# A fused attention and feed-forward kernel: the root's table loaded ahead of the keys' squares, prompt types moved behind a rotation, last products kept in PSUM

## The chip, the cores and the metric

One core of a Trainium2 chip. The metric is the device time of one execution in microseconds; several runs of the kernel are compared by their median. The engines are named TensorE (PE), VectorE (DVE), ScalarE (ACT), POOL (GpSimd) and SyncE (SP); each works through its own instructions in order, and they wait for each other by semaphores.

## The reference

`x` is 64 sequences of 64 tokens of 256 numbers. Cut to what matters:

```python
# block 1: rotate, linear attention with decay, residual
c, s = a * cos(ang), a * sin(ang)          # a = amplitudes ** delta, ang = frequencies * delta
out0, out1 = c * x0 - s * x1, s * x0 + c * x1     # pairs of token rows
q, k, v = split((out @ W_qkv.T).reshape(B, L, 3, 16, 16))   # 64 sequences, 64 tokens, 16 heads of 16
k = (k - mean(k)) * rsqrt(var(k) + 1e-5)   # over each head's 16 numbers
S = sigmoid(log_gamma) * S + v k^T;  y = S q   # scan over the tokens, per head
x = x + y @ W_o.T
# block 2: pooled by a softmax whose mask depends on the prompt type, then a quantized feed-forward
scores = tanh(x @ W1 + b1) @ v
mask = prefix if type == 0 else postfix if type == 1 else all but self
p = softmax(where(mask, scores, -1e30));  pooled = (p @ x) / count(mask)
xq = round(pooled / sx) * sx               # one scale for the whole tensor; weights: one per row
h = quantized(silu(xq @ Wg.T) * (xq @ Wu.T))
x = x + h @ Wd.T
```

## The kernel before

The 4096 tokens are 32 tiles of 128 tokens; four tiles make a group, and there are eight groups (`NG = 8`). All of `x` stays in SBUF. The order of the instructions on TensorE, ScalarE, VectorE and POOL is the order of the code (a schedule written out by hand); SyncE issues most DMAs.

**Preparation.** Constants are built, weights of the attention are turned by TensorE into `wqT`, `wkT`, `wvT`, `woT`, and group 0 is brought up to its scores. `scale_ys(g)` multiplies a group by the sine (POOL, except for group 0), `rotate(g)` adds the cosine part (VectorE, eight instructions, L182 and L185). `gneg`, `gexp`, `gln`, `lgam` make the logarithm of the decay from `log_gamma`; two VectorE products (L777) and an exponential (L788) make the table of decays `gam`. The prompt types of the sequences (`tib`, integers) become numbers `tf` (L756), three selectors `sel` (L761 to L764) and the counts `cnt` (L765, L767): nine VectorE instructions. Nothing of block 2 is needed before the loop.

**Loop over groups.** Pass `p` (1 to 7) projects group `p` and finishes the attention of group `a = p - 1`, while group `q = p - 2` has its pooling. `transposed` copies the transposed inputs from PSUM (ScalarE, L215). `keys(p)` makes the keys on TensorE (`pk`, L225), squares them on ScalarE (L241) and sums the squares per head on VectorE (L242, `ssq`). `weighted` and `diagonal` make `py` and `yT` of group `a` (L384, L400 on ScalarE, L401 on VectorE), `scores` and `decay` make `psc` (L342) and `at` (L367). `key_root(p)` takes the square root on ScalarE (L255), `hidden(q)` a tanh there (`th`, L465), `key_norm(p)` normalises the keys on VectorE (L261 to L273, `kn`), `queries(p)` makes `pq` on TensorE (L302) and `qbd` on ScalarE (L310), `token_scores(q)` makes `psr`, `output` makes `po` (L411), `residual` adds it (L422). Square root and tanh lie in different tables of ScalarE; a load is an instruction of its own, placed by the compiler ahead of the activation that needs another table, unless the code asks for it earlier. Most products live in four PSUM banks that are handed on as their readers finish: `pa` and the first half of `pq` take the banks that the two halves of `yT` are read from, the second half of `pq` takes the bank of `pa` once `th` has read it, `psr` that of the first `pq`, `po` that of the keys' first half once `kn` has read it. In pass 1, where there is no `pa`, the two halves of `pq` take the two banks of `yT`.

**Feed-forward.** After the loop the pooled values are quantized, gate and up products made in a fixed order of steps, then quantized again; `down(g)` multiplies by the down weights into `pdn` (L1229), VectorE applies the scale (L1238) into `res`, the group's result in SBUF. For groups 4 to 7 (`plain`) the residual is added on chip (L1247), by POOL for groups 4 to 6 and by VectorE for group 7, and written out by SyncE (L1248); groups 0 to 3 go out by an adding DMA of POOL's queue (L1251). Group 7 ends with one piece of two tiles and two of one.

Of the kernel before, what the change touches and what calls it, by code (L numbers as in the profile page):

```python
# [15 lines left out]
ALU = mybir.AluOpType  # L16
AX = mybir.AxisListType

P = 128
# [8 lines left out]
def adaln_attn_ffn(  # L28
# [20 lines left out]
    nc = tc.nc  # L49
    B, S, D = x.shape  # L50
# [6 lines left out]
    NN = NT // P  # L57
# [3 lines left out]
    NG = NN // GT  # L61
# [22 lines left out]
    cs, sel, cnt = c32("cs", 2, NN), c32("sel", 3, NN), c32("cnt", NN)  # L84
# [13 lines left out]
    dsc = const.tile([P, D], F32, name="dsc")  # L98
# [22 lines left out]
    with ExitStack() as actx:  # L121
# [37 lines left out]
        def scale_ys(g):  # L159
            if g == 0:  # L160

                ys = pool.tile([P, GT, D], F32, tag="ys", name="ys_0", bufs=1)
                for t in range(GT):
                    nc.scalar.activation(
                        ys[:, t], xg[0][:, t], AF.Copy, scale=cs[:, 1, t : t + 1]
                    )
                T["ys", g] = ys
                return
            tn = slice(g * GT, (g + 1) * GT)
            ys = pool.tile([P, GT, D], F32, tag="ys", name=f"ys_{g}", bufs=1)  # L170
            nc.gpsimd.tensor_tensor(  # L171
                ys, xg[g], cs[:, 1, tn].unsqueeze(2).to_broadcast([P, GT, D]), ALU.mult
            )
            T["ys", g] = ys

        def rotate(g):

            xs, ys = xg[g], T.pop(("ys", g))
            xr = pool.tile([P, GT, D], F32, tag="xr", name=f"xr_{g}", bufs=1)
            for t in range(GT):  # L180
                c = cs[:, 0, g * GT + t : g * GT + t + 1]
                nc.vector.scalar_tensor_tensor(  # L182
                    xr[:, t, 0:P], xs[:, t, 0:P], c, ys[:, t, P:D], ALU.mult, ALU.subtract
                )
                nc.vector.scalar_tensor_tensor(  # L185
                    xr[:, t, P:D], xs[:, t, P:D], c, ys[:, t, 0:P], ALU.mult, ALU.add
                )
            T["xr", g] = xr
# [45 lines left out]
        def keys(g):  # L234

            ssq = pool.tile([P, GT * NH], F32, tag="ssq", name=f"ssq_{g}")
            pks = []
            for r in range(2):
                pk = by_token(g, r, wkT, "pk")
                sq = pool.tile([P, 512], F32, tag="sq", name=f"sq_{g}_{r}")  # L240
                nc.scalar.activation(sq, pk, AF.Square)  # L241
                nc.vector.tensor_reduce(  # L242
                    ssq[:, r * 2 * NH : (r + 1) * 2 * NH],
                    sq.rearrange("p (h e) -> p h e", e=E),
                    AX.X,
                    ALU.add,
                )
                pks.append(pk)
            T["pk", g] = pks, ssq
# [331 lines left out]
        with tc.tile_pool(name="prep", bufs=1) as prep:  # L581
            V = nc.vector

            def p32(name, *free):
                return prep.tile([P, *free], F32, name=name)
# [5 lines left out]
            tib = prep.tile([P, B], I32, name="tib")  # L591
# [16 lines left out]
            for k in range(2):  # L608
                rows = slice(k * A, (k + 1) * A)
# [13 lines left out]
            for k in range(P // 32):  # L623
                rows = slice(32 * k, 32 * (k + 1))
                V.tensor_scalar_add(row[rows], sq32[rows, 0:1], 32.0 * k)
            V.tensor_scalar(ident, col, row, None, ALU.is_equal)
            for k in range(2):
                rows = slice(k * S, (k + 1) * S)
# [20 lines left out]
            lag, npre = p32("lag", S), p32("npre", 2)  # L649
# [14 lines left out]
            rows = bank("rows")  # L664
# [73 lines left out]
            w, pt = turned(wkT, wq_nat, center, 2)  # L738
# [4 lines left out]
            first_transposed(0)  # L743
            w, pt = turned(wqT, wq_nat, ident, 0)
            first_transposed(1)
            V.tensor_copy(w, pt)

            gneg, gexp, gln, lgam = (
                p32(n, NH) for n in ("gneg", "gexp", "gln", "lgam")
            )  # L750
            V.scalar_tensor_tensor(gneg, lgb, -1.0, lgb, ALU.mult, ALU.min)

            tf = p32("tf", NN)
            for k in range(2):
                rows = slice(k * S, (k + 1) * S)
                V.tensor_copy(  # L756
                    tf[rows].rearrange("p (u k) -> p u k", k=2),
                    tib[rows].rearrange("p (u c k) -> p u c k", c=2, k=2)[:, :, k, :],
                )

            V.tensor_single_scalar(sel[:, 0, :], tf, 0.0, ALU.is_equal)  # L761
            V.tensor_single_scalar(sel[:, 1, :], tf, 1.0, ALU.is_equal)
            V.tensor_add(sel[:, 2, :], sel[:, 0, :], sel[:, 1, :])
            V.tensor_scalar(sel[:, 2, :], sel[:, 2, :], -1.0, 1.0, ALU.mult, ALU.add)  # L764
            V.tensor_scalar_mul(cnt, sel[:, 2, :], float(S - 1))  # L765
            for k in range(2):
                V.scalar_tensor_tensor(  # L767
                    cnt, sel[:, k, :], npre[:, k : k + 1], cnt, ALU.mult, ALU.add
                )
            nc.scalar.preload_act_table_set("natural_log_exp_and_others")  # L770
            nc.scalar.activation(gexp, gneg, AF.Exp)
            nc.scalar.activation(gln, gexp, AF.Ln, bias=1.0)
# [22 lines left out]
            w, pt = turned(wvT, wq_nat, ident, 4)  # L795
# [8 lines left out]
                V.tensor_scalar_mul(vb[half, half], ones[half, half], v1s[half])  # L804
            V.tensor_copy(w, pt)
            rotate(1)
            scale_ys(2)
            values(0)
            keys_transposed(0)
# [72 lines left out]
        for step in range(1, NG):  # L882
            p, a, q = step, step - 1, step - 2
            scores(a, 0)
            decay(a, 0)
            if q > 0:
                pooling_out(q - 1)
            T["xT", p] = transposed(T.pop(("xr", p)), p, "xT")
            if q >= 0:
                T["x2T", q, both] = transposed(xg[q], q, "x2T")  # L890
            if p + 1 < NG:
                rotate(p + 1)
                if p + 2 < NG:
                    scale_ys(p + 2)
            keys(p)
            weighted(a, 0)
            diagonal(a, 0)
            scores(a, 1)
            decay(a, 1)
            key_root(p)  # L900
            if q >= 0:
                hidden(q)
            key_norm(p)
            queries(p)
            if q >= 0:
                token_scores(q)
                softmax_exp(q)
            output(a, 0)
            residual(a, 0)
            weighted(a, 1)  # L910
            diagonal(a, 1)
            if q >= 0:
                softmax_div(q)
            mask_bias(a)
            if step == 1:

                nc.scalar.activation(csig, clips, AF.Sigmoid)
            if step < 4:
                weight_scale(step - 1)
            values(p)  # L920
            keys_transposed(p)
            if step < 4:
                weight_round(step - 1)
            if q >= 0:
                weights_transposed(q)
            if 2 <= step < 5:
                weight_widen(step - 2)
            output(a, 1)
            residual(a, 1)
            if q >= 0:  # L930
                pooling(q)
            if 2 <= step < 4:
                weight_transpose(step - 2)
# [76 lines left out]
    with ExitStack() as fctx:  # L1010
# [203 lines left out]
        def down(g):  # L1214
            j, k = divmod(g, 2)

            plain = g >= NG // 2
            res = xg[g - NG // 2 if plain else g]
            at = 0
            for r in range(2):  # L1220
                tiles = slice(2 * r, 2 * r + 2)

                for n in (1, 1) if g == NG - 1 and r else (2,):
                    pdn = ps_d.tile([P, n, D], F32, tag="pdn", name=f"pdn_{g}_{at}")
                    for i in range(n):
                        tok = slice((at + i) * P, (at + i + 1) * P)
                        for c in range(NC):
                            last = c == NC - 1
                            nc.tensor.matmul(  # L1229
                                pdn[:, i, :],  # L1230
                                hq[j][:, NF if last else 2 * c + k, tok],
                                wdT[:, c + k if last else c, :],
                                start=(c == 0),
                                stop=(c == NC - 1),
                            )
                    some = slice(at, at + n)
                    at += n
                    nc.vector.tensor_tensor(  # L1238
                        res[:, some],
                        pdn,  # L1240
                        dsc.unsqueeze(1).to_broadcast([P, n, D]),
                        ALU.mult,
                    )
                    if plain:
                        xr = xg[g][:, some, :]
                        by = nc.gpsimd if g < NG - 1 else nc.vector
                        by.tensor_tensor(xr, xr, res[:, some], ALU.add)  # L1247
                        nc.sync.dma_start(out=ot[g][:, some, :], in_=xr)  # L1248
            if not plain:

                nc.gpsimd.dma_start(out=ot[g], in_=res, accum_op=ALU.add)  # L1251
# [53 lines left out]
```

## Time and profile before

| | |
|---|---|
| runs | 301.86, 301.82, 301.11 us, median 301.82 |
| profiled execution | 301.5 us, span 299.5 us, granted clock 0.998 |
| busy share of the span | TensorE 94%, VectorE 77%, ScalarE 67%, POOL 30% |
| attention loop, passes 1 to 7 | about 28 to 199 us of the span, 24.7 to 25.9 us a pass from pass 2 on |
| down products | about 275.5 to 294.3 us |

The span runs from the first to the last instruction of the profiled execution; 2.0 us lie around it. A line of a timeline gives the start, the time taken, the engine, the line of the code, the operation, output and inputs, and in square brackets how long the engine stood idle before it and who ended that. Where several instructions are merged, `x2` and the like tell how many.

### The profile page before, as it was taken

The page shows a single profiled execution, that of the slowest core. Times are in us where ns is not written, and L with a number is a line of the kernel's source. Part 1 is how long each engine was busy: PE and PEld are TensorE (multiplying, and loading weights), DVE is VectorE, ACT ScalarE, POOL GpSimd, SP SyncE. Part 2 cuts the span into 40 slices and gives each one's busy share as a digit, 9 for nine tenths or more (in the row PEclk, how much of TensorE's full clock was granted, in tenths as well). Part 3 has the DMA queues.
Part 4 walks back from the last instruction along what each step waited for, and adds up shares of the span by engine and source line. Part 5 has one row for each costly group of instructions (what it writes and reads, how often), then busy time and mean ns, then how long its engine had stood idle before and what let it go on. Part 6 is the DMA issues. An engine that isn't in the chain of part 4 may idle for free.

```text
span 299.5 us, 8823 instructions
## 1 busy us (share of the span) xinstructions
PE 280.3 (94%) x3818; PEld 201.7 (67%) x3824; DVE 230.3 (77%) x496; ACT 200.2 (67%) x303; POOL 90.0 (30%) x83
## 2 busy tenths in 40 slices
PE   6999999999999999999999999999879999967993
PEld 5967778668858857875885885777534444434882
DVE  6788885876997697498489557746678999995875
ACT  2785368657684875466358447453489999959990
POOL 0232510600150060045100400016104758850693
PEclk9999999999999999999999999999999999999999
DMA  6596402001000200200000000000000000000796
GB/s 202 158 326 198 143 2 73 2 2 51 25 2 0 74 2 2 71 5 3 0 2 2 2 4 2 0 5 2 2 3 0 0 3 0 0 0 2 109 216 237
DMA packets 14860, 14.50 MB, mean 48 GB/s; under 512 B 1766, under 2 KB 14566, under 8 KB 14822
## 3 DMA queue, kind: packets, MB, share of 16 engines
q1 hardware_dynamic: 12706, 11.84, 12.1%
q0 software_dynamic: 2112, 2.10, 4.7%
q8 instruction: 30, 0.49, 0.7%
q14 instruction: 8, 0.07, 0.1%
q10 hardware_dynamic: 4, 0.00, 0.0%
HBM read 7.65 MB, written 6.29 MB: 47 GB/s over the span
## 4 chain that ended last, share of the span: by engine, by line
PE 74%; ACT 14%; DVE 9%; issue 2%; POOL 0%; POOLq 0%; ACTq 0%; DVEq 0%
PE pv L225 10%; PE po L411 9%; PE pk L225 8%; PE py L384 6%; PE pdn L1229 6%; PE pg L1116 5%; PE pq L302 5%; PE pu L1116 5%; PE psc L342 4%; ACT L255 3%; PE pl L547 3%; ACT L465 3%; PE pxT L212 2%; PE pkT L289 2%; PE idle L659 2%
## 5 line engine op out<-in xcount | busy, mean ns | idle before, releaser
L367 DVE TENSOR_TENSOR at<-psc,gam 128x512 f32<-128x512 f32 x62 | 38.5, 683 | 12.2 <-PE psc L342 12.2
L171 POOL TENSOR_TENSOR ys<-x,cs 128x1024 f32<-128x1024 f32 x7 | 13.3, 1893 | 99.3 <-DVE xr L185 83.5
L302 PE MATMUL pq<-xT,wqT 128*128 128x512 f32 x64 | 31.1, 613 | 1.8 <-ACT th L465 1.8
L411 PE MATMUL po<-woT,yT 128*128 128x256 f32 x128 | 30.2, 380 | 0.0
L225 PE MATMUL pv<-wvT,xT 128*128 128x256 f32 x128 | 29.8, 386 | 0.2 <-ACT qbd L310 0.2
L225 PE MATMUL pk<-wkT,xT 128*128 128x256 f32 x128 | 29.2, 381 | 0.2 <-ACT xT L215 0.2
L225 PEld LDWEIGHTS pv<-wvT,xT 128*128 128x128 f32 x128 | 23.7, 190 | 4.7 <-issue 1.2
L411 PEld LDWEIGHTS po<-woT,yT 128*128 128x128 f32 x128 | 23.7, 190 | 3.5 <-ACT qbd L310 0.5
L225 PEld LDWEIGHTS pk<-wkT,xT 128*128 128x128 f32 x128 | 23.5, 190 | 3.7 <-ACT xT L215 0.9
L1145 DVE TENSOR_REDUCE ham<-hT 128x1 f32<-128x1024 f32 (+1 forms) x25 | 25.9, 1085 | 0.1
L1127 ACT ACTIVATE gate<-pg,wsx 128x1024 f32<-128x1024 f32 (+1 forms) x25 | 25.0, 1013 | 1.3 <-PE pg L1116 1.0
L310 ACT ACTIVATE qbd<-pq,hm 128x512 f32<-128x512 f32 x32 | 20.1, 683 | 8.0 <-PE pq L302 8.0
L1138 POOL TENSOR_TENSOR hT<-gate,up 128x1024 f32<-128x1024 f32 x10 | 23.5, 2362 | 5.5 <-ACT up L1132 5.5
L1116 PE MATMUL pu<-xq,wuT 128*128 128x512 bf16 (+1 forms) x94 | 22.9, 379 | 1.2 <-DVE hT L1140 1.1
L1116 PE MATMUL pg<-xq,wgT 128*128 128x512 bf16 (+1 forms) x94 | 23.0, 381 | 1.0 <-DVE xq L1052 0.9
L1229 PE MATMUL pdn<-wdT,hq 128*128 128x256 bf16 x192 | 22.0, 273 | 2.0 <-DVE hq L1052 1.9
L302 PEld LDWEIGHTS pq<-xT,wqT 128*128 128x128 f32 x64 | 11.0, 189 | 17.8 <-issue 8.6
L1229 PEld LDWEIGHTS <-hq 128*128 128x128 bf16 x192 | 18.3, 98 | 5.9 <-DVE hq L1052 3.8
L400 ACT ACTIVATE yT<-py,hm 128x256 f32<-128x256 f32 x32 | 13.4, 470 | 11.3 <-PE py L384 11.3
L401 DVE SCALAR_TENSOR_TENSOR yT<-py,hm,yT 128x256 f32<-128x256 f32 x32 | 14.0, 480 | 8.7 <-ACT yT L400 8.4
L342 PE MATMUL psc<-qbd,kT 32*64 32x128 f32 x1024 | 20.2, 279 | 0.5 <-ACT kT L292 0.3
L241 ACT ACTIVATE sq<-pk 128x512 f32<-128x512 f32 x16 | 9.5, 596 | 16.0 <-PE pk L225 16.0
(203 smaller groups left out, 556.1 us busy)
## 6 DMA issues: line engine op xcount, KB each, us to landing
x<-in_x_dram SPq DMA_DIRECT2D x7, 512.0 KB, 7.3
out_dram<-x SPq DMA_DIRECT2D x4, 512.0 KB, 4.7
out_dram<-x POOLq DMA_DIRECT2D x4, 512.0 KB, 6.9
out_dram<-x SPq DMA_DIRECT2D x7, 256.0 KB, 4.1
wq_nat<-in_L_attn_W_qkv_dram SPq DMA_DIRECT2D x3, 256.0 KB, 4.0
wnat_d<-in_L_ffn_w_down_dram SPq DMA_DIRECT2D x1, 704.0 KB, 6.3
wnat<-in_L_ffn_w_gate_dram SPq DMA_DIRECT2D x1, 640.0 KB
wnat<-in_L_ffn_w_up_dram SPq DMA_DIRECT2D x1, 640.0 KB, 5.7
```

The source lines that it names most:

```text
L225: nc.tensor.matmul(pk[:, i * D : (i + 1) * D], xT[:, kc, t * P : (t + 1) * P], w[:, kc, :], start=(kc == 0), stop=(kc == 1),)
L302: nc.tensor.matmul(pq, wqT[:, kc, hf * P : (hf + 1) * P], xT[:, kc, :], start=(kc == 0), stop=(kc == 1),)
L310: nc.scalar.activation(qbd[:, hf, :, k, :], pq.rearrange("p (b s) -> p b s", s=S), AF.Copy, scale=hm[:, k : k + 1],)
L342: nc.tensor.matmul(banks[p][k * S : (k + 1) * S, i, hf, :], kT[rows, hf, b * S : (b + 1) * S], qbd[rows, hf, b].rearrange("p k t -> p (k t)"),
L367: nc.vector.tensor_tensor(dst, scores, by, ALU.mult)
L384: nc.tensor.matmul(pys[k][32 * p : 32 * p + 32, i, hf, :], v[half, 2 * r + i, pair * 2 * E : (pair + 1) * 2 * E], at[half, p, i, hf].rearr ...
L411: nc.tensor.matmul(po[:, i * D : (i + 1) * D], yT[:, i, hf].rearrange("p k t -> p (k t)"), woT[:, hf, :], start=(hf == 0), stop=(hf == 1),)
L1116: nc.tensor.matmul(dst[:, k, :] if wide else dst[k * LAST : (k + 1) * LAST, 0, :], w[:, kc, c * P : min((c + 1) * P, FF)], xq[:, kc, g * G ...
L1127: nc.scalar.activation(gates[i], pgu.pop(("g", i)), AF.Silu, scale=wsx[:, 0, c : c + 1])
L1138: nc.gpsimd.tensor_tensor(hs[i], gates.pop(i), ups.pop(i), ALU.mult)
L1145: nc.vector.tensor_reduce(ham[:, i : i + 1], hs.pop(i), AX.XY, ALU.max, apply_absolute_value=True)
L1229: nc.tensor.matmul(pdn[:, i, :], hq[j][:, NF if last else 2 * c + k, tok], wdT[:, c + k if last else c, :], start=(c == 0), stop=(c == NC ...
```

## The change

Three edits. In the preparation `gneg` is computed ahead of the copy of `wqT`, and the nine instructions on the prompt types move from there to the place behind `rotate(1)`, ahead of `scale_ys(2)` in the code. In each pass of the loop ScalarE is told to load the table of the square root ahead of `keys(p)`. In the last group the scaled products are written back into PSUM, over the unscaled ones, and the sum reads them there.

```diff
             first_transposed(1)
-            V.tensor_copy(w, pt)
 
             gneg, gexp, gln, lgam = (
                 p32(n, NH) for n in ("gneg", "gexp", "gln", "lgam")
             )
             V.scalar_tensor_tensor(gneg, lgb, -1.0, lgb, ALU.mult, ALU.min)
-
-            tf = p32("tf", NN)
-            for k in range(2):
-                rows = slice(k * S, (k + 1) * S)
-                V.tensor_copy(
-                    tf[rows].rearrange("p (u k) -> p u k", k=2),
-                    tib[rows].rearrange("p (u c k) -> p u c k", c=2, k=2)[:, :, k, :],
-                )
-
-            V.tensor_single_scalar(sel[:, 0, :], tf, 0.0, ALU.is_equal)
-            V.tensor_single_scalar(sel[:, 1, :], tf, 1.0, ALU.is_equal)
-            V.tensor_add(sel[:, 2, :], sel[:, 0, :], sel[:, 1, :])
-            V.tensor_scalar(sel[:, 2, :], sel[:, 2, :], -1.0, 1.0, ALU.mult, ALU.add)
-            V.tensor_scalar_mul(cnt, sel[:, 2, :], float(S - 1))
-            for k in range(2):
-                V.scalar_tensor_tensor(
-                    cnt, sel[:, k, :], npre[:, k : k + 1], cnt, ALU.mult, ALU.add
-                )
+            V.tensor_copy(w, pt)
             nc.scalar.preload_act_table_set("natural_log_exp_and_others")
...
             V.tensor_copy(w, pt)
             rotate(1)
+
+            tf = p32("tf", NN)
...
             scale_ys(2)
             values(0)
...
                 rotate(p + 1)
                 if p + 2 < NG:
                     scale_ys(p + 2)
+
+            nc.scalar.preload_act_table_set("sqrt_and_others")
             keys(p)
             weighted(a, 0)
...
-                    nc.vector.tensor_tensor(
-                        res[:, some],
-                        pdn,
-                        dsc.unsqueeze(1).to_broadcast([P, n, D]),
-                        ALU.mult,
+
+                    y, by = (
+                        (res[:, some], nc.gpsimd) if g < NG - 1 else (pdn, nc.vector)
+                    )
+                    nc.vector.tensor_tensor(
+                        y, pdn, dsc.unsqueeze(1).to_broadcast([P, n, D]), ALU.mult
                     )
                     if plain:
                         xr = xg[g][:, some, :]
-                        by = nc.gpsimd if g < NG - 1 else nc.vector
-                        by.tensor_tensor(xr, xr, res[:, some], ALU.add)
+                        by.tensor_tensor(xr, y, xr, ALU.add)
                         nc.sync.dma_start(out=ot[g][:, some, :], in_=xr)
```

The lines behind `tf = p32("tf", NN)` in the new place are the removed ones, unchanged.

More of the change, by code (lines that the diff above doesn't have):

```diff
@@ L806, in adaln_attn_ffn @@
             rotate(1)
+            tf = p32("tf", NN)
+            for k in range(2):
+                rows = slice(k * S, (k + 1) * S)
+                V.tensor_copy(
+                    tf[rows].rearrange("p (u k) -> p u k", k=2),
+                    tib[rows].rearrange("p (u c k) -> p u c k", c=2, k=2)[:, :, k, :],
+                )
+            V.tensor_single_scalar(sel[:, 0, :], tf, 0.0, ALU.is_equal)
+            V.tensor_single_scalar(sel[:, 1, :], tf, 1.0, ALU.is_equal)
+            V.tensor_add(sel[:, 2, :], sel[:, 0, :], sel[:, 1, :])
+            V.tensor_scalar(sel[:, 2, :], sel[:, 2, :], -1.0, 1.0, ALU.mult, ALU.add)
+            V.tensor_scalar_mul(cnt, sel[:, 2, :], float(S - 1))
+            for k in range(2):
+                V.scalar_tensor_tensor(
+                    cnt, sel[:, k, :], npre[:, k : k + 1], cnt, ALU.mult, ALU.add
+                )
             scale_ys(2)
@@ L1237, in down @@
                     at += n
+                    y, by = (
+                        (res[:, some], nc.gpsimd) if g < NG - 1 else (pdn, nc.vector)
+                    )
                     nc.vector.tensor_tensor(
-                        res[:, some],
-                        pdn,
-                        dsc.unsqueeze(1).to_broadcast([P, n, D]),
-                        ALU.mult,
+                        y, pdn, dsc.unsqueeze(1).to_broadcast([P, n, D]), ALU.mult
                     )
```

## The prediction

> **What bounds the kernel now.** I read the totals first, then who waited for whom on TensorE, then the timelines of the three places that the change touches. From the page's totals and from the waits of TensorE:
>
> ```profile
> PE 280.3 (94%) x3818; PEld 201.7 (67%) x3824; DVE 230.3 (77%) x496; ACT 200.2 (67%) x303; POOL 90.0 (30%) x83
> ```
> ```profile
> PE pq L302 <- ACT th L465: 1.8, 6, 0.3
> ...
> PE pv L225 <- ACT qbd L310: 0.2, 1, 0.2
> ```
>
> TensorE is busy 94% of the span. An edit on another engine therefore pays only where TensorE waits for that engine, or after TensorE's last matmul, and it costs wherever it makes TensorE wait anew. The second view has two waits in reach: 1.8 us over six passes of the attention loop (0.29 to 0.30 each) for the tanh `th`, and 0.18 us once for the first `qbd`. ScalarE in pass p = 4, from its timeline:
>
> ```profile
> 102.87 1.09 ACT L215 COPY x2T<-px2T 128x512 f32<-128x512 f32 x2
> 104.96 0.60 ACT L241 ACTIVATE sq<-pk 128x512 f32<-128x512 f32 x1 [0.99 <-PE pk L225]
> 106.69 0.60 ACT L241 ACTIVATE sq<-pk 128x512 f32<-128x512 f32 x1 [1.13 <-PE pk L225]
> 107.71 0.84 ACT L400 ACTIVATE yT<-py,hm 128x256 f32<-128x256 f32 x2 [0.43 <-PE py L384]
> 108.57 1.28 ACT L255 ACT_TABLE_LOAD   x1
> 109.86 0.35 ACT L255 ACTIVATE root<-ssq,lneps 128x64 f32<-128x64 f32 x1
> 110.23 1.28 ACT L465 ACT_TABLE_LOAD   x1
> 111.53 0.47 ACT L465 ACTIVATE th<-pa,b1s 128x256 f32<-128x256 f32 x1
> ```
>
> Two table loads stand between `yT` and `th`; the first square has 0.99 us of idle time ahead of it. At the start, VectorE and POOL (timeline of the first 36 us):
>
> ```profile
> 12.49 1.89 POOL L171 TENSOR_TENSOR ys<-x,cs 128x1024 f32<-128x1024 f32 x1 [11.99 <-DMA x<-in_x_dram]
> 13.43 0.99 DVE L751 SCALAR_TENSOR_TENSOR gneg<-lgb 128x16 f32<-128x16 f32 x1
> 14.34 0.35 DVE L756 CAST tf<-tib 64x32 f32<-64x32 int32 x2
> ...
> 16.15 0.17 DVE L775 SCALAR_TENSOR_TENSOR lgam<-lgb,gln 128x16 f32<-128x16 f32 x1
> ...
> 18.87 1.14 DVE L261 TENSOR_SCALAR var<-ssq 128x64 f32<-128x64 f32 x1
> ...
> 27.37 1.89 POOL L171 TENSOR_TENSOR ys<-x,cs 128x1024 f32<-128x1024 f32 x1 [6.22 <-DVE xr L185]
> ```
> ```profile
> 28.44 2.48 DVE L367 TENSOR_TENSOR at<-psc,gam 128x512 f32<-128x512 f32 x4 [1.21 <-PE psc L342]
> ...
> 35.11 0.88 DVE L401 SCALAR_TENSOR_TENSOR yT<-py,hm,yT 128x256 f32<-128x256 f32 x2 [0.22 <-ACT yT L400]
> ```
>
> `gneg`, 128 x 16 elements, takes 0.99 us and ends at 14.42, just as POOL's `ys` ends at 14.38; `var` takes 1.14 us beside POOL's select of `gam` (from 18.81), and 0.19 as the median of its eight runs. So a VectorE instruction on SBUF operands can stand still until POOL is done. The end, VectorE and then what the DMA engines moved (last columns: DMA share, GB/s):
>
> ```profile
> 293.03 0.69 DVE L1238 TENSOR_TENSOR x<-pdn,dsc 128x512 f32<-128x512 f32 x1 [0.62 <-PE pdn L1229]
> 293.76 1.33 DVE L1247 TENSOR_TENSOR x<-x,x 128x512 f32<-128x512 f32 x1
> ```
> ```profile
> 297.00:297.30 0.30, 0.00 (x0) 0.00 (x0) 0.00 (x0) 0.00 (x0) 0.00 (x0) 1.00 0.95 335
> 297.30:297.60 0.30, 0.00 (x0) 0.00 (x0) 0.00 (x0) 0.00 (x0) 0.00 (x0) 1.00 0.44 140
> 297.60:297.90 0.30, 0.00 (x0) 0.00 (x0) 0.00 (x0) 0.00 (x0) 0.00 (x0) 1.00 0.97 338
> ```
>
> The sum at 293.76 reads two SBUF tensors while POOL adds (its last sum runs from 293.27 to 294.54), and takes 1.33 us.
>
> **The change part by part: the root's table.** The load of 1.28 us leaves the place ahead of `root` and goes behind the copies of `x2T`. In p = 4 it runs from 103.98 to 105.26; the first square starts there instead of at 104.96 and ends at 105.86. Queued behind the load on ScalarE are both squares; VectorE's sums of them (L242) wait for the first. Those start at 106.85, after the rotation, so 0.30 us costs nothing; in p = 3, where the idle stretch is 0.74 us, the first square ends at 80.34 and VectorE asks at 80.95. The second square waits for TensorE as before (106.69). `root` then follows `yT` directly, tanh's load and `th` come 1.28 us earlier, `th` ends at 110.72 instead of 112.00. TensorE's second half of `pq` uses the PSUM bank that `th` reads; it waited 0.29 us for it and has now 1 us to spare. What is late next: `po` takes the bank of the first half of `kn` (p = 3: 87.31 + 0.69 = 88.00), and TensorE would come there at 88.52 - 0.29 = 88.23. That holds by 0.23 us, so the whole wait goes: 6 x 0.29 = -1.74 us. Pass p = 1 has no tanh and gains nothing; it found the root's table loaded already, and a repeated load of 1.28 would fit into its 1.71 us of idle time ahead of the squares.
>
> A rule speaks against this part: the Trainium skill, "ScalarE: Activation LUTs", section "What ACT_TABLE_LOAD costs", gives a switch 1283 ns for the load and about 1380 ns more for a drain, 2.66 us together. The rows show the load alone: `yT` ends at 108.55, the load starts at 108.57 and ends at 109.85, `root` starts at 109.86. I take 1.28; by the page's figure, used as an estimate, six passes would lose about what the edits win and the time would come to 301.6.
>
> **The prompt types.** `gneg` moves ahead of the copy of `wqT`: it then runs at about 11.9, before POOL's `ys` starts, once `log_gamma` has landed (SyncE's queue saw that by 10.79). Nine VectorE instructions (two casts, two compares, an add, four more for `sel` and `cnt`) leave the stretch from 14.34 to 16.15. The table load behind `gneg` ends at 15.14 either way, `gln` at 15.62; `lgam` starts at 15.66 instead of 16.15. The decays `gam` are then ready at 17.15, their exponential waits for the second square (ends at 17.31) and starts 0.37 us earlier than 17.68. The root's load, `root` and `qbd` move with it. TensorE, however, is busy until 21.89 with `pw_woT` ahead of `pv` at 22.07: it wins 0.18 us, not 0.37.
>
> The nine instructions now follow rotate(1) on VectorE, whose last piece starts at 26.89 - 0.37 = 26.52; the first cast comes 0.26 us on, at 26.78. Undisturbed they take 16.15 - 14.34 = 1.81 us, to 28.59. But POOL's next `ys` starts 0.14 us after that rotation (27.37 behind 27.23), now at 27.00, and holds to 28.89. The two casts pass by about 27.15, the first compare stands until 28.89 as `gneg` and `var` did, and the rest takes 1.33 us (second compare 14.82 to 16.15): VectorE is free at about 30.20. Queued behind on VectorE: four `at` (2.40 us from start to start), rotate(2) (2.10), two sums of squares (1.27) and the first half of `yT` (0.44), some 6.15 with their overlaps. `yT` is then half done at 36.35 instead of 35.55. The first half of `pq` takes its bank, and TensorE started `pq` at 35.65 before; it now starts at 36.40. The bank is the wait that takes the place of the old one: +0.75 us in place of -0.18. Bounds: -0.18 where nothing blocks (`yT` then waits for ScalarE as before), +1.2 if even the first compare has to run again behind POOL. I take +0.75, by the two blocked rows. Two further users have slack: POOL's mask needs `sel` at 35.01, and SyncE's load of the gate weights, which waits for the preparation's memory and went at 24.45, goes at about 30; VectorE reads it at 43.50, and all DMA traffic of the start is over by some 37 us, 43 with the whole delay.
>
> **The last group.** The products stay in PSUM, the sum reads PSUM and one SBUF tensor. That form stands in the trace: the residual L422, 128 x 512, 0.69 us; and L1238 takes 0.69 beside a running POOL. So 1.33 becomes 0.69, and the last sum ends at 296.04 instead of 296.68. No row shows VectorE writing PSUM; it costs between nothing and the slowest row, 0.64 us more, and I take nothing, since all its rows that read PSUM take 0.69. Of the 0.64 us most is lost behind the DMA engines: POOL's sums set their work from 295.47 on, they are full until 297.38, wait, and move the last 128 KB from 297.55 to 297.98. Directly queued, these end at about 297.78: -0.20 us, bounds 0 and -0.64.
>
> Sum: -1.74 + 0.75 - 0.20 = -1.19 us. The profiled execution took 301.5 (span 299.5 and 2.0 around it), so 300.3; the median of the runs is 0.3 above the profiled one, the lowest 0.4 below. I forecast 300.4.
>
> **Rivals.** (1) POOL does not hold VectorE up: the small instructions come one behind the other and POOL gets its turn after them, or the casts hold the way. Then 301.5 - 0.18 - 1.74 - 0.20 = 299.4. For it: most `var` rows are short. Against it: `gneg` and `var`, both of the kinds moved. 0.18. (2) Slower: the load ahead of the squares holds ScalarE longer than its record. In p = 4, load end + two squares (1.12) + a sum (0.69) + half of `yT` (0.44) must be done when TensorE wants that bank for `pa`, about 108.76. That holds up to a load of 2.5 us (2.2 in p = 3); beyond it each excess counts six times, and from 2.65 us on the kernel is slower. At 2.96 us, the stretch that the two loads and the root between them take now (108.57 to 111.53), it is 6 x 0.48 + 0.26 = 3.1 us worse, 303.4. Against it: seven loads of 1.28 without a gap on either side. 0.10. (The page's figure in the Trainium skill falls on this mechanism, at its break-even.) (3) The root's edit brings nothing: VectorE comes 0.3 us later than now with `kn` and `po` waits for it, or the load is made again ahead of `root`. Against the latter: in p = 1 `root` runs at 35.33 without a load, behind squares and copies that kept the table of 19.23. Then 301.5 + 0.75 - 0.20 = 302.05. 0.14. The forecast keeps 0.58.
>
> **The numbers.** About 0.3%, 0.9 us, is what a measurement of this kernel can tell from no change. Of the forecast's 0.58 some 0.46 lies more than 0.9 below and 0.12 nearer; with (1) faster is 0.64. (2) is slower for 0.09, same for 0.01; (3) same for 0.12, slower for 0.02. Same 0.25, slower 0.11. From 299.3 to 302.1 the range takes in (1), (3) and the bounds of the unknown costs; (2) is left out.
>
> **What would show it.** In the loop: L255 loads at once behind `x2T`, no wait of `pq` for `th`, `th` 1.28 us earlier against `yT`. At the start: `lgam` near 15.7, `pv` near 21.9, one of the compares 1.7 us long beside POOL, `at` near 30.2, `pq` near 36.4 with a wait for `yT` of 0.9. At the end: sum of 0.69, no gap in the DMA work at 297.4. A short row for all compares makes it rival 1; a `pa` that waits for `yT` in every pass makes it rival 2.

## The result and the profile after

The changed kernel takes 300.17 us as the median of nine runs (299.59 to 300.95), the kernel before 301.75 (301.07 to 302.13): a ratio of 0.9952, 95% interval 0.9938 to 0.9966, which makes it 1.45 us faster (the two medians differ by 1.58). The forecast was 300.4 us, from a sum of -1.19 us. The profiled execution is the longest of the nine, 300.95 us at a span of 299.0; the spans of the others run from 297.6 to 298.6. So the profiles are compared place by place here, and not by their ends.

The busy time of the engines, and who kept TensorE waiting at `pq`:

```profile
PE 280.2 (94%) x3818; PEld 202.2 (68%) x3824; DVE 230.1 (77%) x496; ACT 201.5 (67%) x304; POOL 90.0 (30%) x83
```
```profile
PE pq L302 <- DVE yT L401: 1.0, 1, 1.0
```

The 1.8 us of waits for `th` are gone, and so is the 0.2 of `pv` for `qbd`; one wait of 1.0 us for `yT` is new. ScalarE in pass p = 4 (timeline):

```profile
103.31 1.09 ACT L215 COPY x2T<-px2T 128x512 f32<-128x512 f32 x2
104.42 1.28 ACT L896 ACT_TABLE_LOAD   x1
105.72 0.60 ACT L241 ACTIVATE sq<-pk 128x512 f32<-128x512 f32 x1
...
108.15 0.84 ACT L400 ACTIVATE yT<-py,hm 128x256 f32<-128x256 f32 x2 [0.43 <-PE py L384]
108.88 0.35 ACT L255 ACTIVATE root<-ssq,lneps 128x64 f32<-128x64 f32 x1
109.25 1.28 ACT L465 ACT_TABLE_LOAD   x1
110.54 0.47 ACT L465 ACTIVATE th<-pa,b1s 128x256 f32<-128x256 f32 x1
```

The load runs between the copies and the first square, the root follows `yT`, and `th` ends 2.9 us after the start of `yT` (111.01 and 108.15), against 4.3 before (112.00 and 107.71). That is 1.43 us less, a little more than the load's 1.28: without the load in between, `root` starts 0.11 us before `yT` has ended. From the scores of pass 2 to those behind pass 7 TensorE takes 198.24 - 49.51 = 148.73 us, against 199.01 - 48.34 = 150.67.

The start (timeline of 9 to 37 us, all engines):

```profile
11.77 0.17 DVE L750 SCALAR_TENSOR_TENSOR gneg<-lgb 128x16 f32<-128x16 f32 x1
...
16.03 0.17 DVE L757 SCALAR_TENSOR_TENSOR lgam<-lgb,gln 128x16 f32<-128x16 f32 x1 [2.14 <-ACT gln L754]
...
22.11 3.62 PE L225 MATMUL pv<-wvT,xT 128*128 128x256 f32 x16
...
27.28 1.89 POOL L171 TENSOR_TENSOR ys<-x,cs 128x1024 f32<-128x1024 f32 x1 [6.21 <-DVE xr L185]
27.45 1.76 DVE L798 TENSOR_SCALAR sel<-tf 128x32 f32<-128x32 f32 x1
...
30.45 2.48 DVE L367 TENSOR_TENSOR at<-psc,gam 128x512 f32<-128x512 f32 x4
...
36.13 0.86 DVE L401 SCALAR_TENSOR_TENSOR yT<-py,hm,yT 128x256 f32<-128x256 f32 x2
36.65 0.30 PEld L302 LDWEIGHTS pq<-xT,wqT 128*128 128x128 f32 x2 [1.26 <-DVE yT L401]
```

`gneg` takes 0.17 us where it took 0.99. The first compare of the prompt types, 128 x 32 elements, takes 1.76 us: it ends at 29.21, just behind POOL's `ys` at 29.17. All that VectorE does next is late, and TensorE starts `pq` at 36.65, 1.0 us later than before.

The end, on VectorE:

```profile
292.82 0.69 DVE L1249 TENSOR_TENSOR x<-pdn,x 128x512 f32<-128x512 f32 x1
```

The sum takes 0.69 us instead of 1.33, and the last one ends at 295.10. The DMA engines are full from 294.6 to 296.7, without the pause that lay ahead of the last piece before; how they end is shown with the experiments.

### The profile page after: what moved, and what is told of

Same layout as the page of the kernel before. It is cut to its first block, busy times and chain, and to the rows that moved or that the text cites. A ratio compares the mean times of both kernels' runs of the same rounds, so it can differ in the third digit from the quotient of the medians.

```text
span 299.0 us, 8824 instructions
## 1 busy us (share of the span) xinstructions
PE 280.2 (94%) x3818; PEld 202.2 (68%) x3824; DVE 230.1 (77%) x496; ACT 201.5 (67%) x304; POOL 90.0 (30%) x83
## 3 DMA queue, kind: packets, MB, share of 16 engines
q1 hardware_dynamic: 12706, 11.84, 12.3%
HBM read 7.65 MB, written 6.29 MB: 47 GB/s over the span
## 4 chain that ended last, share of the span: by engine, by line
PE 75%; DVE 16%; ACT 5%; issue 2%; POOL 0%; DVEq 0%; POOLq 0%; ACTq 0%
PE po L411 10%; PE pv L225 9%; PE pk L225 8%; PE pq L302 6%; PE pdn L1231 6%; PE py L384 6%; PE pg L1118 5%; PE pu L1118 5%; PE psc L342 5%; DVE at L367 3%; PE pl L547 3%; PE pxT L212 2%; PE pkT L289 2%; PE pa L456 2%; PE idle L659 2%
## 5 line engine op out<-in xcount | busy, mean ns | idle before, releaser
L411 PE MATMUL po<-woT,yT 128*128 128x256 f32 x128 | 30.8, 385 | 0.1
L302 PE MATMUL pq<-xT,wqT 128*128 128x512 f32 x64 | 29.5, 604 | 1.0 <-DVE yT L401 1.0
L322 ACT COPY v<-pv 128x512 f32<-128x512 f32 x16 | 9.4, 584 | 16.3 <-PE pv L225 16.3
```

Of the source, the lines that this page charges most:

```text
L302: nc.tensor.matmul(pq, wqT[:, kc, hf * P : (hf + 1) * P], xT[:, kc, :], start=(kc == 0), stop=(kc == 1),)
L411: nc.tensor.matmul(po[:, i * D : (i + 1) * D], yT[:, i, hf].rearrange("p k t -> p (k t)"), woT[:, hf, :], start=(hf == 0), stop=(hf == 1),)
```

## Experiments

All ratios are to the kernel before, with their 95% intervals. Differences in us between two versions are worked out from their ratios.

**The three parts alone.** Each is the kernel before with one part of the change's diff.

The root's table:

```diff
+            nc.scalar.preload_act_table_set("sqrt_and_others")
             keys(p)
```

> The kernel before with the root's table loaded ahead of the keys' squares, nothing else. Theory (TensorE waits for th six times, the load hides under the idle time ahead of the squares): no wait of pq for th is left, every pass from 2 to 7 is 0.29 us shorter or a little more, -1.74 us by the waits, up to -1.95 by the landmarks of the changed kernel; ratio 0.9935 to 0.9945. Rival (the gain of the whole change came from the start or the tail): ratio above 0.998.

299.84 us, ratio 0.9944 (0.9925 to 0.9963), 1.7 us faster. The waits for `th` are gone. The table's load alone gives 0.2 us more than the whole change does, which is less than the intervals.

`gneg` and the prompt types:

```diff
+            V.scalar_tensor_tensor(gneg, lgb, -1.0, lgb, ALU.mult, ALU.min)
             V.tensor_copy(w, pt)
...
             rotate(1)
+            tf = p32("tf", NN)
+            ...
```

> The kernel before with gneg ahead of wqT and the prompt types behind rotate(1), nothing else. Theory (the first compare stands until POOL's ys is done, at comes 2 us late, pq waits for yT): slower by 1.0 to 1.2 us, ratio 1.0030 to 1.0040, with a wait of pq for yT of 1.0 us and the compare at 1.7 us. Rival (the late at is absorbed further on, or the earlier decays pay for it): ratio 0.998 to 1.001.

301.99 us, ratio 1.0009 (0.9999 to 1.0019): 0.3 us slower at the best estimate, not the 1.0 to 1.2 that the theory gave. Its waits, though, are the expected ones:

```profile
PE pq L302 <- ACT th L465: 1.8, 6, 0.3
PE pq L302 <- DVE yT L401: 1.0, 1, 1.0
```

So 1.0 us is lost at `pq`, and something else gives most of it back. It is the start: `pv` begins at 21.03 in this profile and not at 22.07, and `pq`, for all its waiting, at 35.57 and not at 35.65. TensorE reached the keys `pk` at 12.36 instead of 13.05, because it sped up earlier. The same weight loads for the same tile, before and here:

```profile
L706 PEld LDWEIGHTS pw_wkT<-center,wq_nat x8: 333/333/333, 9.1 to 10.6; 128*128 128x128 f32 x8
```
```profile
L706 PEld LDWEIGHTS pw_wkT<-center,wq_nat x8: 192/192/334, 9.1 to 10.1; 128*128 128x128 f32 x8
```

(minimum, median and maximum in ns.) In every profile TensorE begins with loads of 333 ns and goes over to 192; the moment lies near 9.5 us here and near 12.3 in the profile of the changed kernel. With `gneg` early, `pv` starts 8.67 us behind the start of `pk`, whenever that is: 12.36 and 21.03 here, 13.44 and 22.11 in the changed kernel. With the old order VectorE holds `pv` at 21.96 to 22.30 (four profiles), however early TensorE is ready: `gneg` stands until POOL's `ys` is done and ends 0.03 or 0.04 us behind it, at 14.30 to 14.65; the nine instructions and `lgam` follow it, behind them come ScalarE's exponential, the root and `qbd`, and `pv` starts 7.65 or 7.66 us behind the end of `gneg` in all four. So the early `gneg`, with the nine instructions out of its way, is worth from hardly anything to 1.0 us, as the execution has it. Ten profiles with the new order have `pv` at 21.39 on average (21.02 to 22.11), four with the old one at 22.08: 0.7 us.

The last group:

```diff
-                    nc.vector.tensor_tensor(res[:, some], pdn, ..., ALU.mult)
+                    nc.vector.tensor_tensor(y, pdn, ..., ALU.mult)   # y = pdn in the last group
-                        by.tensor_tensor(xr, xr, res[:, some], ALU.add)
+                        by.tensor_tensor(xr, y, xr, ALU.add)
```

> The kernel before with the last group's products left in PSUM, nothing else. Theory (the DMA engines are full behind POOL's last sum, so of 0.64 us on VectorE only some 0.2 reach the end): ratio 0.9990 to 0.9998, the last sum ends 2.4 - 0.64 us after TensorE's last matmul, the DMA data without the gap ahead of the last piece. Rival (the last issue sets the end): -0.64 us, ratio 0.9975 to 0.9982.

301.72 us, ratio 0.9999 (0.9986 to 1.0012). No gain shows, though the 0.2 us of the theory (0.9993) lie within the interval. The last sum ends 0.6 us earlier against TensorE's last matmul, but from the last sum to the end of the span it takes 4.15 us instead of 2.82.

**Moving the prompt types into a gap of VectorE.** The changed kernel, with the nine instructions in pass 1:

```diff
                 weight_scale(step - 1)
+            if step == 1:
+                prompt_types()      # the nine instructions; tib, tf, npre kept past the preparation
+                mask_bias(a)
```

> The changed kernel with the nine instructions on the prompt types moved on into pass 1, behind weight_scale(0), where VectorE stood idle for 2.8 us and POOL has nothing to do; the mask of group 0 follows them. Theory: no compare is held up, at starts at about 28.3, pq does not wait for yT, the wait of 1.0 us and the 0.15 of py behind kn are gone: 1.1 us faster than the changed kernel, ratio to before 0.991 to 0.992. Rival (the types were not what made pq wait): ratio as the changed kernel's, 0.995.

298.76 us, ratio 0.9907 (0.9891 to 0.9922): 1.4 us faster than the changed kernel; no version that computes everything has a lower ratio. `pq` starts at 34.94 and waits for nobody. One thing differs from what was expected: POOL is not idle beside the nine. It begins the mask of group 0 at 45.50, as soon as two selectors are there; the add, one of the next two and the last pair take 0.62, 0.53 and 1.29 us instead of 0.19, 0.18 and 0.54, and the nine take 3.4 us again (44.88 to 48.26). Here that delays no product of TensorE, since VectorE had the time to spare.

**Taking POOL away instead.** The types stay behind `rotate(1)`; ScalarE makes the next `ys`:

```diff
-            if g == 0:
+            if g in (0, 2):        # four scaled copies on ScalarE
...
-            scale_ys(2)
             values(0)
             keys_transposed(0)
+            scale_ys(2)
```

> The changed kernel with group 2's product with the sine made by ScalarE behind kT instead of by POOL behind rotate(1); the prompt types stay where the change put them. Theory (it is POOL's ys that holds the first compare): the compare takes 0.2 us instead of 1.76, at starts near 28.9, pq waits for yT for less than 0.1 us; 1.0 to 1.2 us faster than the changed kernel, ratio to before 0.991 to 0.992. Rival (nine instructions at this place are too many by themselves, whoever else runs): the wait of pq stays above 0.5 us and the ratio at 0.994 to 0.995.

299.09 us, ratio 0.9914 (0.9901 to 0.9928). VectorE's timeline:

```profile
26.94 0.18 DVE L799 TENSOR_SCALAR sel<-tf 128x32 f32<-128x32 f32 x1
...
28.36 2.48 DVE L368 TENSOR_TENSOR at<-psc,gam 128x512 f32<-128x512 f32 x4
```

The same compare at the same place takes 0.18 us instead of 1.76 once POOL has nothing to do, and the wait at `pq` is gone. So nine instructions were not too many at this place; POOL beside them was.

**Holding ScalarE longer ahead of the squares.** The changed kernel with one or two further loads:

```diff
+            nc.scalar.preload_act_table_set("natural_log_exp_and_others")
             nc.scalar.preload_act_table_set("sqrt_and_others")
             keys(p)
```

> The changed kernel with a second table load (of the logarithm's table) directly ahead of the root's in each pass: ScalarE is held 2.57 us ahead of the squares. Theory of the prediction (TensorE loses what goes beyond 2.5 us, 2.2 in pass 3, six times over): 0.5 to 1.1 us slower than the changed kernel, ratio to before 0.9968 to 0.9990, with short waits of pa for yT. Rival (loads ahead of the squares cost nothing, or a drain of over 1 us comes with each): no difference, or 7 us and more.

301.16 us, ratio 0.9994 (0.9983 to 1.0004): 1.3 us behind the changed kernel, a little more than expected, with intervals of about half a microsecond. Its profile shows two waits that the changed kernel lacks, 0.4 us of `pa` for `yT` and 0.2 of `po` for `kn`, each once.

> The changed kernel with two more table loads ahead of the root's in each pass: ScalarE is held 3.85 us. Theory of the prediction: 6 x (3.85 - 2.48) + 0.26 = 8.5 us slower than the changed kernel, ratio to before 1.023, each load 1.28 us without a gap, pa waiting for yT by over 1 us in six passes. Rival (as above): no difference, or over 14 us.

308.69 us, ratio 1.0239 (1.0215 to 1.0264): 8.65 us behind the changed kernel where 8.5 was expected. Its waits:

```profile
PE pa L456 <- DVE yT L401: 8.6, 6, 1.7
```

The loads stand back to back, 1.28 us each (107.13, 108.41 and 109.70 in pass 4), and what goes beyond the slack of some 2.5 us is paid six times by `pa`: 1.65 us in pass 3 and 1.35 to 1.40 in the others, where the theory has 1.63 and 1.37.

**The change without the types' part.** The kernel before with the table's load and the last group's products:

> The kernel before with the table's load and the last group's products as changed; gneg and the prompt types as before. Theory (types cost 1.0 us at pq, and gneg early wins some 0.5 to 0.8 because TensorE then starts pv as soon as it is free): ratio 0.994 to 0.995, within 0.3 us of the changed kernel, and 1.0 us slower than the version with the types in pass 1. Rival (gneg early wins 0.2 us at most, as predicted): ratio 0.9915 to 0.9925.

299.40 us, ratio 0.9924 (0.9910 to 0.9938). This is the rival's range, 0.8 us faster than the changed kernel, while the types alone cost only 0.3 against the kernel before. Both hold together at about half a microsecond. The gain from the early `gneg` is not refuted by it: in this profile TensorE was fast early (`pk` at 12.36) and stood idle for 0.80 us ahead of `pv`, waiting for `qbd`, and that is what an early `gneg` would have saved.

**What holds up the end.** Three versions of the one with the types in pass 1: the last group as before; the last two pieces issued by ScalarE's queue; groups 0 to 3 written without adding.

```diff
-                        nc.sync.dma_start(out=ot[g][:, some, :], in_=xr)
+                        q = nc.scalar if g == NG - 1 and r else nc.sync
+                        q.dma_start(out=ot[g][:, some, :], in_=xr)
```
```diff
-                nc.gpsimd.dma_start(out=ot[g], in_=res, accum_op=ALU.add)
+                nc.gpsimd.dma_start(out=ot[g], in_=res)
```

> The version with the prompt types in pass 1, with the last group's edit undone (products in SBUF as before). Theory (the 0.64 us that the edit wins on VectorE is lost again because one of the 16 DMA engines is 0.4 to 0.8 us behind the others and sets the end): ratio to before as with the edit, 0.9900 to 0.9920, and a tail of 2.8 to 3.0 us from the last sum to the end of the span instead of 3.7. Rival (the edit wins 0.6 us together with the others): ratio 0.9925 to 0.9935.

> The version with the prompt types in pass 1, the last two pieces of 128 KB issued from ScalarE's queue instead of SyncE's. Theory A (the lagging DMA engine has its backlog from what came before, whichever queue the last pieces use): the trickle of one engine after the others remains, ratio as without, 0.990 to 0.992. Theory B (the lag comes from the order in one queue): the trickle is gone and the span is 0.4 to 0.6 us shorter, ratio 0.989.

> The version with the prompt types in pass 1, where groups 0 to 3 are written by POOL's queue without adding to what lies in memory (their sum with x is left out). Theory (the adding writes are what one DMA engine falls behind on): no trickle of one engine at the end, tail from the last sum to the end of the span 3.1 to 3.3 us instead of 3.7. Rival (the lag has another source): tail and trickle as with adding.

The last of them was run a second time:

> The version with the prompt types in pass 1 and plain writes of groups 0 to 3 once more (their sum with x is left out), since one of eight profiles with adding writes and the last group's edit ends without a lagging engine too. Theory (the adding writes make one DMA engine lag): no trickle of one engine at the end, tail 3.3 to 3.4 us, ratio 0.988 to 0.9895. Rival (the lag comes and goes, whatever the writes): a trickle, or a ratio of 0.990 to 0.992 as with adding.

| version | us | ratio | last sum to end of span |
|---|---|---|---|
| types in pass 1 | 298.76 | 0.9907 (0.9891 to 0.9922) | 3.68 |
| the same, last group as before | 298.98 | 0.9912 (0.9893 to 0.9931) | 3.00 |
| the same, ScalarE's queue | 299.26 | 0.9908 (0.9886 to 0.9930) | 4.20 |
| the same, plain writes | 298.25 | 0.9888 (0.9867 to 0.9910) | 3.32 |
| the same again | 298.36 | 0.9894 (0.9873 to 0.9915) | 3.32 |

Neither undoing the last group's edit nor another queue for the last pieces makes a difference beyond the intervals, and with ScalarE's queue one engine still works on alone for about 1 us at the end. With the edit and adding writes the tail is 3.42 to 4.59 us in eight profiles, without the edit 2.82 to 3.00 in four. Counted from TensorE's last matmul, the way to the end is 5.2 to 6.4 us in these eight, 5.2 to 5.5 in these four, and 5.05 with plain writes: beside adding writes the edit shortens nothing. The DMA engines of the changed kernel and then of the version with plain writes at their ends (busy times of the engines, granted clock, and in the last two columns DMA share and GB/s):

```profile
296.70:297.00 0.30, 0.00 (x0) 0.00 (x0) 0.00 (x0) 0.00 (x0) 0.00 (x0) 0.50 0.42 140
297.00:297.30 0.30, 0.00 (x0) 0.00 (x0) 0.00 (x0) 0.00 (x0) 0.00 (x0) 0.50 0.07 24
297.30:297.60 0.30, 0.00 (x0) 0.00 (x0) 0.00 (x0) 0.00 (x0) 0.00 (x0) 0.50 0.06 20
```
```profile
294.60:294.90 0.30, 0.00 (x0) 0.00 (x0) 0.00 (x0) 0.00 (x0) 0.00 (x0) 0.50 0.39 130
294.90:295.20 0.30, 0.00 (x0) 0.00 (x0) 0.00 (x0) 0.00 (x0) 0.00 (x0) 0.50 0.00 0
```

A share of 0.06 is one engine of 16. In the changed kernel that one works on for 0.6 us after the others. Seven of the eight profiles with the edit and adding writes end so (the eighth, of the version with two loads, has the shortest tail, 3.42); neither of the two with plain writes does, and their tails are 3.32 both times. Before the change the pause ahead of the last piece (the share of 0.44 at 297.30) comes first, and the engines end together. So a lagging engine takes what the edit wins.

Are the adding writes what makes it lag? The experiment alone does not prove it: the plain writes are 0.4 to 0.6 us faster in total with intervals that overlap those of the adding version. The traces show when the lag begins, and it is older than the last group. Each engine ends its part of each of POOL's four writes of 512 KB with a packet of 4 bytes. In all twelve profiles with adding writes, the kernel before among them, the last engine ends its part of the first three writes at most 0.11 us behind the next to last, and its part of the fourth 0.6 to 2.4 us behind. Within 1.5 us of the end of the third write, one packet of 16 KB of the queue that loads instructions (q8) goes by and takes an engine 0.9 to 2.0 us; in the changed kernel it starts at 288.56 and takes 1.17. With plain writes that packet comes too, and again one engine ends what follows it, a piece of 256 KB, 0.6 us behind the others (0.7 in the second run; share 0.06 or 0.07 from 286.5 to 286.9). But there the engines stand idle between the pieces (share 0.00 at 288.4 to 288.6), and from the next piece on the last one is 0.03 us behind at most. So the traces point at the instruction packet as the start of the lag, and at the adding writes, with which the engines stay full until about 294 in the changed kernel, as what leaves no pause to catch up in; the edit then removes the last such pause. This is read from the order of events: no run moves the packet, and the profile does not tell which engine carries it.

## Why the prediction was right

**The root's table** was right in place and size: -1.74 us from six waits, -1.7 measured alone, and -1.94 between the landmarks of the loop. It hid where the prediction put it: the first square came some 0.3 us later against the copies, as forecast, and the sums, the second square and `yT` did not. The slack given for it, 2.5 us, holds too, for the three loads cost what the formula says. `po` did not begin to wait for `kn`.

**The drain** that the Trainium skill adds to a load ("ScalarE: Activation LUTs", section "What ACT_TABLE_LOAD costs") does not appear: in these profiles three loads in a row take 1.28 us each with no gap, and the table's load alone wins what a load of 1.28 would leave. The 0.15 us by which `th` gained more than 1.28 is all that could be counted as more than the load itself.

**The prompt types.** The hold-up by POOL came as forecast: a compare of 1.76 us (1.7 forecast), `at` at 30.45 (30.20 forecast) and `pq` at 36.65 (36.40 forecast). The 0.25 us between forecast and result have one source: the root started 0.09 us earlier than before, not 0.37, as TensorE reached the keys later in that execution. Another 0.15 us went where the prediction had seen slack: `kn` was late enough that `py` started at 42.09 behind it, 1.23 us long instead of 1.16.

**The step that was mis-sized** is "it wins 0.18 us", at `pv`. It took the start of `pk` from the one profile as fixed; that moves by 1.1 us between executions. And it read TensorE as busy until 21.89, the end of `pw_woT` as modelled, while in the profiles with the new order `pv` starts 0.16 us before that end: by the 8.67 us behind `pk`, even this one profile had 0.35 us to win. On average the early `gneg` is worth 0.7 us. With it the part costs 1.0 + 0.1 - 0.7 = 0.4 us; 0.75 was forecast, and the two direct comparisons give 0.3 and 0.8. Two more pairs of versions differ in the early `gneg` and have no wait of `pq`: types in pass 1 against the change without the types' part (0.9907 and 0.9924, 0.5 us), and the same with the last group as before against the table's load alone (0.9912 and 0.9944, 1.0 us). Their mean agrees with 0.7, each with an interval of over half a microsecond.

**The last group** was sized at -0.2 us with bounds 0 and -0.64; the best estimate is 0 (0.9999), at the bound, and 0.2 is not excluded. The prediction saw that the DMA engines were full, but it read their mean share as if all 16 ended together.

**The total** is nearer than its terms: with some -1.7, +0.4 and 0 in place of -1.74, +0.75 and -0.20, the third of a microsecond by which the types cost less and the 0.2 that the last group did not bring offset each other. That is luck; the place and the sign of the two larger terms are not.

## What to carry to other kernels

When a run of small instructions is moved on an engine, look at what the other engines do at its new place: the nine here take 1.8 us alone and 3.4 beside one POOL instruction, and the fix was a gap 18 us further on that had room even for 3.4. A table load is free as long as what is queued behind it is done before another engine asks for it; here that slack was computed beforehand as 2.5 us, and with three loads the waits came out within a tenth of a microsecond a pass. A mean share of DMA engines hides the one that ends last.

## What the runs showed of the hardware

TensorE's first matmuls run slower: weight loads of 333 ns against 192, one every 0.21 us against one every 0.11. The moment of the change moved from about 9.5 to 12.3 us between executions, though TensorE had its first loads at 2.8 us in each, while the granted clock in the profile's rows stays at 1.00 from 0 to 15 us. The Trainium skill, "TensorE: Matmul & The Clock Gate", section "Part 1: The HAM clock gate", describes a clock gate that opens after a busy window of about 3.4 us; the window is free-running, so that the moment varies, by 0.5 us either way. A step at a moment that varies agrees with it, but the step comes 6.7 to 9.5 us behind the first loads here and varies by 2.8 us, more than the page gives.

VectorE instructions of a fifth of a microsecond stood until the POOL instruction beside them was done: `gneg`, 128 x 16 elements, took 0.93 to 1.60 us in the four profiles with the old order and 0.17 in the ten with the new one, and the first compare 1.76 us beside POOL's `ys` and 0.18 without it.

One of the 16 DMA engines can end well after the others, in the changed kernel by 0.6 us: so in seven of eight profiles with adding writes and the last group's edit, in none of two with plain writes. In all fourteen an engine falls behind at about the time of one 16 KB packet of instructions; whether that packet is the cause stays open.
